# Layer 2's expert matrices: transposes one expert ahead with copies on ScalarE, and the second pair's answers added inside its own parts

## The chip, the cores and the metric

The kernel runs on one core of one Trainium2 chip. A core has five engines that matter here: TensorE (PE in the profile; PEld is its weight load), VectorE (DVE), ScalarE (ACT), GpSimd (POOL) and SyncE (SP), which here only issues transfers. The metric is the device time of one execution in microseconds (us), given as the median of several runs.

## The reference

Four layers work on one array x of 2048 tokens with 128 numbers each, seen as four blocks of 512 tokens. Each layer is a "macaron": half of a mixture of experts, an attention, half of the same mixture again, each on a normalized x and added to x. The change touches the seam between the second mixture of layer 0 and the first of layer 1, and a matrix product that prepares layer 2.

```python
x = x + 0.5 * _L0_ffn_ref(_layernorm(x), ...)      # 8 experts, one per token
x = x + 0.5 * _L1_ffn_ref(_layernorm(x), ...)      # 8 small experts, 2 per token, and a shared one
x = x + _L1_attn_ref(_layernorm(x), ...)
x = x + 0.5 * _L2_ffn_ref(_layernorm(x), ...)
```

Layer 2's experts have no nonlinearity between their two matrices: `h = xt @ w_in[e].T` and then `gates[:, e] * (h @ w_out[e].T)`. The two matrices of an expert can therefore be multiplied once, `w_in[e].T @ w_out[e].T`, to a single 128 x 128 matrix, and the mixture needs only that.

## The kernel before, in words

A token row of 128 numbers lies in one SBUF partition; a block of 512 tokens is a tile of 128 partitions by 4 rows. Layer 0's experts gather their tokens by transfers through DRAM, compute, and send each weighted answer row back to a DRAM array `res` with indirect transfers from GpSimd (`experts`, lines 418 to 523). `combine(b)` (lines 525 to 532) then loads the answers of block b from there with one transfer on SP into a tile of tag `n` of the pool `work`, which has three buffers, and adds them to x on VectorE.

Layer 1's mixture works on pairs of blocks. `l1_ffn` (line 1078) first calls `normed_T` (line 1042): `norms` takes the statistics of eight tiles of 128 tokens on VectorE (lines 160 and 161), the inverse root on GpSimd as a power (line 165), and the normalization alternately on VectorE (line 178) and ScalarE (line 174), into two tiles of the same tag `n`. TensorE transposes them (line 187, tile T_f), ScalarE copies the result out (nT_f, line 1049). Then follow the gate's logits (line 1058), the products with the up matrices (lines 1092 and 1093), the sigmoid on ScalarE (line 1096), two multiplications on VectorE (lines 1097 and 1098), the choice of two experts per token as a row of small VectorE operations (`route`, lines 216 to 226, and lines 1104 to 1115), the transposed gates (line 1071), their way through DRAM (lines 1075 and 1124), a multiplication by them on GpSimd (line 1147) and the down products (line 1135). `followed` puts behind the first pair's mixture the start of layer 1's attention for block 0.

`prep_l2` loads layer 2's weights and builds the eight expert matrices `m`. Its loads are issued one expert at a time during layer 0's experts, into a tile `raw` that fills with both matrices of all experts. After the experts' last product, its last part runs: for each expert four transposes of 128 x 128 into one PSUM bank (line 1275), a copy of 128 x 512 out of it (wo2T, line 1277), four accumulating products (line 1280) into another bank, and a copy of 128 x 128 into `m` (line 1283). Both copies go through a helper, `copy` (lines 131 to 136), that alternates between VectorE and ScalarE from call to call. The pool that holds `raw` ends with this part, so what is later placed in its room waits for the last product: GpSimd's memset of `vpad` (line 574) is the first such.

The order of the work has two sources. Where a block of code stands under `manual_schedule`, the four compute engines keep the order of the code: all of layer 1's attention is so written. Outside of it, as here, a planner lays out each engine's instructions in advance: it prefers what comes first in the code, and fills an engine that it reckons idle with later work that it reckons ready, by its own estimate of durations. On the chip each engine then keeps that order. `skewed(gens, lag)` (line 1468) sets the order of the code: in each round it takes one part of every generator, and the generator number i joins in round i x lag.

Of the kernel before, what the change touches and what calls it, by code (L numbers as in the profile page):

```python
# [9 lines left out]
FP = mybir.dt.float32  # L10
# [7 lines left out]
P = 128  # L18
D = 128
NB, S = 4, 512  # L20
# [3 lines left out]
E = 8  # L24
# [4 lines left out]
FF = 512  # L29
NC = FF // P  # L30
# [11 lines left out]
def kernel(ctx: ExitStack, tc: tile.TileContext, a: dict, out: bass.AP):  # L42
    nc = tc.nc
# [9 lines left out]
    def const(shape, name, dtype=FP):  # L53
        return cpool.tile(shape, dtype, name=name, tag=name)

    def bank(name):
        return psum.tile([P, 512], FP, name=name, tag="bank", bufs=8)
# [14 lines left out]
    ident = const([P, P], "ident")  # L72
# [46 lines left out]
    def load(ap, shape, name):  # L119
        t = pools["w"].tile(shape, FP, name=name, tag=name)  # L120
        nc.sync.dma_start(t, ap)
        return t

    def load_row(ap, name, tag=None):
        t = pools["w"].tile([P, D], FP, name=name, tag=tag or name)
        nc.sync.dma_start(t, ap.partition_broadcast(P))
        return t
# [3 lines left out]
    def copy(dst, src):  # L131
        n_copies[0] += 1
        if n_copies[0] % 2:
            nc.vector.tensor_copy(dst, src)
        else:
            nc.scalar.copy(dst, src)

    def load_T(ap, rows, cols, name, tag=None):

        dst = pools["w"].tile([cols, rows], FP, name=name, tag=tag or name)  # L140
        m = min(rows, P)
        k = rows // m
        raw = stage.tile([m, k, cols], FP, name=f"raw_{name}", tag="raw")
        nc.sync.dma_start(raw, ap.rearrange("(k m) c -> m k c", m=m))
        ps = bank(f"ps_{name}")
        for i in range(k):
            nc.tensor.transpose(ps[:cols, i * m : (i + 1) * m], raw[:, i, :], ident[:m, :m])
        copy(dst, ps[:cols, :rows])
        return dst
# [422 lines left out]
    def padded(pool, i):  # L572
        v = pool.tile([P, NT, NH, SLOT], FP, name=f"vpad{i}", tag=f"vpad{i}", bufs=1)
        nc.gpsimd.memset(v, 0.0)
        nc.gpsimd.memset(v[:, :, :, HD : HD + 1].rearrange("p t h o -> p (t h o)"), 1.0)
        return v
# [668 lines left out]
    def prep_l2(pool):  # L1245

        l2["gate"] = load_T(a["L2_ffn_w_gate"], E, D, "gate2T")
        l2["w_in"] = load(a["L2_attn_W_in"], [P, 2 * D], "win2")
        l2["w_out"] = load(a["L2_attn_W_out"], [P, D], "wout2")
        l2["b_out"] = load_row(a["L2_attn_b_out"], "bout2")  # L1250
        l2["b_in"] = load_T(a["L2_attn_b_in"].rearrange("(k d) -> k d", k=2), 2, D, "bin2T")
        yield

        m = pools["w"].tile([P, E, D], FP, name="m2", tag="m2")
        l2["m"] = m
        got = {}

        def fetch(e):
            wi, wo = raw[:, 0, e].rearrange("p (c d) -> p c d", d=D), raw[:, 1, e]
            nc.sync.dma_start(wi, a["L2_ffn_w_in"][e].rearrange("(c f) d -> f c d", f=P))  # L1260
            nc.sync.dma_start(wo, a["L2_ffn_w_out"][e])
            got[e] = wi, wo

        raw = pool.tile([P, 2, E, FF], FP, name="raw2", tag="raw2")
        for e in range(E):

            behind = yield
            nc.gpsimd.tensor_copy(raw[0:1, :, e, 0], behind[0:1, 0:1].to_broadcast([1, 2]))
            fetch(e)
        yield  # L1270
        for e in range(E):
            wi, wo = got[e]
            ps = bank(f"wo2T_{e}")
            for c in range(NC):
                nc.tensor.transpose(ps[:, c * P : (c + 1) * P], wo[:, c * P : (c + 1) * P], ident)
            woT = pool.tile([P, FF], FP, name=f"wo2T_{e}", tag="woT", bufs=3)
            copy(woT, ps)
            pm = bank(f"m2_{e}")
            for c in range(NC):
                nc.tensor.matmul(  # L1280
                    pm[:, :D], wi[:, c, :], woT[:, c * P : (c + 1) * P], start=(c == 0), stop=(c == NC - 1)
                )
            copy(m[:, e, :], pm[:, :D])

    def l2_ffn(pool, i, bs):
        tag = f"f2{i}_{bs[0]}"
# [95 lines left out]
    def prep_l3_ffn(behind):  # L1382
        l3["w"] = yield from moe_weights("L3_ffn", "l3", behind)
        l3["gate"] = wpool.tile([P, E], FP, name="gate3", tag="gate3")
        nc.sync.dma_start(l3["gate"], a["L3_ffn_wg"])
# [78 lines left out]
    def whole(parts):  # L1464
        for _ in parts:
            pass

    def skewed(gens, lag):

        live = {i: g for i, g in enumerate(gens)}  # L1470
        r = 0
        while live:
            for i in list(live):
                if r >= i * lag and next(live[i], "end") == "end":
                    del live[i]
            r += 1
            yield
# [19 lines left out]
    pairs = [[b, b + 1] for b in range(0, NB, 2)]  # L1497
    gate0T = wpool.tile([D, E], FP, name="gate0T", tag="gate0T")
    ps = bank("gate0T")
    nc.tensor.transpose(ps[:, :E], gate0, ident[:E, :E])  # L1500
    nc.vector.tensor_copy(gate0T, ps[:, :E])
    with tc.tile_pool(name="tables", bufs=1) as tables:
# [17 lines left out]
        f01 = Mixture("f01", CAP0, 1)  # L1520
# [3 lines left out]
    with tc.tile_pool(name="weights12", bufs=1) as mid:  # L1524
        pools["w"] = mid
        prep_l1()
        with tc.tile_pool(name="raw2", bufs=1) as pool:
            made = prep_l2(pool)
            next(made)
            next(made)  # L1530
            f01.experts(l0["w"], made.send)
            whole(made)
        first = small.tile([P, 1], FP, name="first_sigmoid", tag="first_sigmoid", bufs=1)
        nc.scalar.activation(first, l2["m"][:, 0, 0:1], AF.Sigmoid)
        for b in range(NB):
            whole(f01.combine(b))
        with tc.tile_pool(name="ahead1", bufs=2) as ahead:
            vpads[:] = [padded(ahead, 0), None]
            begun = l1_begin(ahead)

            def followed(pool, bs):
                yield from l1_ffn(pool, 0, bs)
                if bs[0] == 0:

                    yield from begun[0](0)
                    for g in range(2):
                        begun[1](0, g)
                        yield
                        begun[4][0, g] = begun[2](0, g)

            with tc.tile_pool(name="ffn10", bufs=2) as pool:
                whole(skewed([followed(pool, bs) for bs in pairs], 12))

            l1_attn(lambda pool: prep_l3_ffn(xs[0]), begun)

        def behind(pool, bs):
            yield from l1_ffn(pool, 1, bs)
            yield from l2_ffn(pool, 0, bs)
            yield from l2_attn(pool, bs)
            yield from l2_ffn(pool, 1, bs)  # L1560
            if bs[0] == 0:

                parts = f30.tokens(bs, l3["gate"], "scalar", pool, apart=True)
                while next(parts, "end") != "end" and next(parts, "end") != "end":
                    yield
            else:
                yield from skewed([f30.tokens([b], l3["gate"], "scalar", pool) for b in bs], 3)

        with tc.tile_pool(name="chain", bufs=2) as pool:
            decay = pool.tile([P, S], FP, name="decay", tag="decay", bufs=1)  # L1570
            nc.gpsimd.memset(decay, 0.9)
            for bs in pairs:
                l2["gates", bs[0]] = pool.tile([P, 2 * NT, P], FP, name=f"gates{bs[0]}", tag=f"gates{bs[0]}", bufs=1)
                nc.gpsimd.memset(l2["gates", bs[0]], 0.0)

            l2["row"] = []
            for u in range(E // 4):
                flag = pool.tile([P, 1], FP, name=f"flag{u}", tag=f"flag{u}", bufs=1)
                nc.vector.tensor_reduce(flag, ident.rearrange("p (r c) -> p r c", c=SLOT)[:, :, u], AX.X, ALU.add)
                row = pool.tile([P, P], FP, name=f"row{u}", tag=f"row{u}", bufs=1)  # L1580
                nc.vector.tensor_copy(row, flag.to_broadcast([P, P]))
                l2["row"].append(row)
            with tc.manual_schedule(engines={mybir.EngineType.Pool}):
                whole(skewed([behind(pool, bs) for bs in pairs], 8))
        pools["w"] = wpool
# [54 lines left out]
```

## Time and profile before

| | us |
|---|---|
| median of the timed runs | 1533.77 (1532.04 to 1535.4, 3 runs) |
| the profiled execution | 1513.06 |
| its span, first to last instruction | 1511.3 |
| TensorE busy in the span | 1271.2 (84%) |
| VectorE / ScalarE / GpSimd busy | 880.3 / 682.8 / 694.0 |
| stretch from layer 0's last product to T_f, 419.6 to 443.5 | 23.9 |
| TensorE / VectorE / ScalarE busy in it | 12.93 / 14.06 / 6.15 |

The profile shows one execution. Its times count from the first instruction; a group or a chain piece is named by engine, the tile that it writes and the line of the kernel. "Idle before" is the time in which the engine had nothing running ahead of an instruction, with what released it. The mean TensorE clock granted over the span was 0.911 of full speed, and 1.00 in the stretch from 419.6 to 443.5.

### The profile page before, as it was taken

What the parts mean: (1) busy time and instruction counts of PE and PEld (TensorE: products, weight loads), DVE (VectorE), ACT (ScalarE), POOL (GpSimd) and SP (SyncE); (2) the same over time, 40 slices, a digit from 0 to 9 for tenths busy, and PEclk for the clock granted to TensorE, in tenths of its full rate; (3) what the DMA queues carried; (4) which work ended last, traced back from release to release, by engine and by line L of the source; (5) the groups of instructions that cost most, each with busy time, mean ns of one, the idle gap of its engine ahead of it and who ended that gap; (6) DMA issues with size and microseconds to landing.
All of it is one profiled execution on the core that took longest, in us unless ns stands there. A gap on an engine that the chain in (4) does not pass through costs nothing.

```text
span 1511.3 us, 28774 instructions
## 1 busy us (share of the span) xinstructions
PE 1271.2 (84%) x10645; PEld 816.7 (54%) x10645; DVE 880.3 (58%) x2890; ACT 682.8 (45%) x1431; POOL 694.0 (46%) x808
## 2 busy tenths in 40 slices
PE   4787999995969999999878878729689999998394
PEld 3465666774746666667555656616433333333173
DVE  5236767763355657767456566525367787774343
ACT  1235877871422367767522222103236655564042
POOL 5346767871433678868323111464431223312343
PEclk9897999995999999999999888759879999999597
DMA  9410240002513884231022000023105000000223
GB/s 262 101 53 22 79 170 12 9 7 73 151 37 65 223 258 145 87 121 44 4 64 49 1 1 1 28 71 91 60 15 177 15 7 10 14 3 15 78 78 112
DMA packets 100660, 106.21 MB, mean 70 GB/s; under 512 B 9084, under 2 KB 73832, under 8 KB 100520
## 3 DMA queue, kind: packets, MB, share of 16 engines
q1 hardware_dynamic: 91752, 90.11, 20.7%
q0 software_dynamic: 6656, 13.22, 2.5%
q8 instruction: 84, 1.38, 0.4%
q10 hardware_dynamic: 2112, 1.05, 0.3%
q14 instruction: 56, 0.46, 0.1%
HBM read 62.49 MB, written 41.85 MB: 69 GB/s over the span
## 4 chain that ended last, share of the span: by engine, by line
PE 70%; DVE 9%; POOL 8%; DMA 5%; issue 5%; ACT 3%; SPq 1%; POOLq 0%; ACTq 0%; DVEq 0%
PE s_a L610 13%; PE t_a L655 10%; PE o_f L515 6%; PE h_f L479 6%; PE acc_a L677 5%; PE acc_a L749 5%; PE y_f L1329 3%; PE t_a L610 3%; POOL disp_f L408 2%; PE ot_a L768 2%; PE gu_f L1092 2%; PE lg_f L322 1%; POOL rstd_f L165 1%; DVE low L699 1%; PE gu_f L1093 1%
## 5 line engine op out<-in xcount | busy, mean ns | idle before, releaser
L642 POOL TENSOR_SCALAR sc_a<-sc_a,top_a 128x128 f32<-128x128 f32 (+3 forms) x256 | 274.8, 1089 | 84.7 <-DVE top_a L627 55.8
L610 PE MATMUL s_a<-k_a,q_a 32*128 32x512 f32 (+3 forms) x1536 | 263.4, 544 | 7.0 <-DVE top_a L631 3.7
L719 ACT ACTIVATE w_a<-t_a 128x512 f32<-128x512 f32 x256 | 140.4, 595 | 116.6 <-PE t_a L610 86.9
L699 DVE TENSOR_REDUCE low<-s_a 128x1 f32<-128x512 f32 x256 | 163.4, 684 | 45.4 <-PE t_a L610 32.7
L655 PE MATMUL t_a<-ident,sc_a 128*128 128x128 f32 x1280 | 174.3, 283 | 4.3 <-DVE top_a L631 3.8
L610 PE MATMUL t_a<-ql_a,k_a 32*128 32x512 f32 x512 | 167.2, 644 | 0.3 <-DVE low L699 0.2
L501 POOL DMA_INDIRECT res_f<-y_f,back_f x112 | 109.8, 980 | 124.6 <-ACT y_f L500 90.3
L655 PEld LDWEIGHTS t_a<-ident,sc_a 128*128 128x128 f32 x1280 | 144.6, 144 | 41.0 <-issue 16.5
L644 ACT ACTIVATE sc_a<-sc_a,top_a 128x128 f32<-128x128 f32 (+3 forms) x256 | 135.0, 575 | 12.8 <-DVE top_a L631 12.2
L610 PEld LDWEIGHTS s_a<-k_a,q_a 32*128 32x128 f32 x1536 | 91.5, 187 | 79.1 <-issue 41.9
L664 ACT ACTIVATE w_a<-t_a 128x256 f32<-128x256 f32 (+2 forms) x192 | 94.2, 526 | 71.0 <-PE t_a L655 70.8
L408 POOL DMA_INDIRECT disp_f<-n_f,to_f x96 | 94.8, 988 | 56.2 <-issue 35.8
L515 PE MATMUL o_f<-w_l,h_f 128*128 128x128 f32 (+1 forms) x896 | 109.6, 277 | 0.0
L515 PEld LDWEIGHTS o_f<-w_l,h_f 128*128 128x128 f32 (+1 forms) x896 | 102.1, 184 | 8.0 <-DVE back_f L464 4.4
L479 PE MATMUL h_f<-dT_f,w_l 128*128 128x320 f32 (+1 forms) x256 | 104.1, 544 | 2.8 <-ACT dT_f L457 2.8
L677 PE MATMUL acc_a<-w_a,vpad 128*32 128x128 f32 x2560 | 98.2, 280 | 0.0
L666 ACT COPY w_a<-t_a 128x256 f32<-128x256 f32 (+2 forms) x192 | 93.5, 527 | 5.0 <-PE t_a L655 4.7
L631 DVE CUSTOM_DVE_ANT_0 sc_a<-s_a,future 128x128 f32<-128x128 f32 (+3 forms) x128 | 62.3, 487 | 47.7 <-PE s_a L610 39.0
L1147 POOL TENSOR_TENSOR h_f<-h_f,cb_f 128x512 f32<-128x512 f32 x32 | 40.7, 1286 | 104.4 <-DVE h_f L1098 62.7
L631 DVE CUSTOM_DVE_ANT_0 sc_a<-s_a,table 128x128 f32<-128x128 f32 (+3 forms) x128 | 62.3, 487 | 43.5 <-PE s_a L610 38.3
L500 ACT ACTIVATE y_f<-o_f,d_f 128x128 f32<-128x128 f32 (+1 forms) x112 | 39.0, 394 | 98.0 <-DVE o_f L495 94.1
L749 PE MATMUL acc_a<-w_a,vpad 128*32 128x256 f32 x1024 | 82.1, 391 | 1.0 <-DVE low L699 0.9
(341 smaller groups left out, 2182.8 us busy)
## 6 DMA issues: line engine op xcount, KB each, us to landing
fac_a<-fac_a_sb SPq DMA_DIRECT2D x36, 256.0 KB, 4.9
disp_f<-zeros_f SPq DMA_DIRECT2D x4, 2080.0 KB, 10.6
d_f<-disp_f SPq DMA_DIRECT2D x32, 260.0 KB, 3.0
w_l<-in_L_ffn_w_dram SPq DMA_DIRECT2D x16, 512.0 KB, 7.2
cb_f<-rows_f SPq DMA_DIRECT2D x16, 512.0 KB, 8.4
q_a<-fac_a SPq DMA_DIRECT2D x32, 256.0 KB, 3.5
k_a<-fac_a SPq DMA_DIRECT2D x32, 256.0 KB, 3.8
r_f<-res_f SPq DMA_DIRECT2D x16, 256.0 KB, 2.8
```

The source lines that it names most:

```text
L408: nc.gpsimd.indirect_dma_start(out=self.to[c][i0 + t][:, :], out_offset=bass.IndirectOffsetOnAxis(ap=to[:, c, t : t + 1], axis=0), in_=ns[ ...
L479: nc.tensor.matmul(ps[u][:, :cap], w1[:, e, (c + u) * P : (c + u + 1) * P], dT, start=True, stop=True)
L515: nc.tensor.matmul(po[:m, s, :], h[:, c, s * P : s * P + m], w2[:, e, c, :], start=(c == 0), stop=(c == NC - 1),)
L610: nc.tensor.matmul(ps[:, n0:n1], q[r : r + SLOT, i * P : (i + 1) * P], k[r : r + SLOT, n0:n1], start=True, stop=True)
L631: nc.vector.tensor_tensor_reduce(sc, banks[r][:, :n], more, -1.0, HUGE, ALU.add, ALU.min, top)
L642: nc.gpsimd.tensor_scalar(sc, sc, top, None, ALU.subtract)
L644: nc.scalar.activation(sc, sc, AF.Exp, bias=top, scale=-1.0)
L655: nc.tensor.transpose(ps[:, x * n + j * P : x * n + (j + 1) * P], st["sc", u, i, r0 + x][:, j * P : (j + 1) * P], ident,)
L677: nc.tensor.matmul(st["acc", u][r * SLOT : (r + 1) * SLOT, i * P : (i + 1) * P], vpads[b % 2][:, j, g * 4 + r, :], st["w", u, i, r][:, j * ...
L699: nc.vector.tensor_reduce(st["low", u][:, i, c : c + 1], ps, AX.X, ALU.max, negate=True)
L719: nc.scalar.activation(w, ps, AF.Exp)
L749: nc.tensor.matmul(acc[r * SLOT : (r + 1) * SLOT, n0:n1], vpads[b % 2][:, j, g * 4 + r, :], st["w", u, j, r][:, n0:n1], start=(j == 0 and ...
```

## The change

Two edits. In `prep_l2`, the loop runs one round more than there are experts. In round e it transposes expert e's matrix and copies it, and then forms the product of expert e - 1. The code order on TensorE is thus T0, T1, P0, T2, P1, ... where it was T0, P0, T1, P1. Both copies are called on ScalarE directly and no longer go through the alternating helper.

In the main part, `combine` runs ahead of layer 1 for the first pair of blocks only. The second pair's two `combine` calls become the first two parts of its own generator `followed`, and the lag of the second generator goes from 12 rounds to 10, so that its `l1_ffn` begins in round 12, as before.

```diff
-        for e in range(E):
-            wi, wo = got[e]
-            ps = bank(f"wo2T_{e}")
-            for c in range(NC):
-                nc.tensor.transpose(ps[:, c * P : (c + 1) * P], wo[:, c * P : (c + 1) * P], ident)
-            woT = pool.tile([P, FF], FP, name=f"wo2T_{e}", tag="woT", bufs=3)
-            copy(woT, ps)
-            pm = bank(f"m2_{e}")
-            for c in range(NC):
-                nc.tensor.matmul(
-                    pm[:, :D], wi[:, c, :], woT[:, c * P : (c + 1) * P], start=(c == 0), stop=(c == NC - 1)
-                )
-            copy(m[:, e, :], pm[:, :D])
+        wT = {}
+        for e in range(E + 1):
+            if e < E:
+                ps = bank(f"wo2T_{e}")
+                for c in range(NC):
+                    nc.tensor.transpose(ps[:, c * P : (c + 1) * P], got[e][1][:, c * P : (c + 1) * P], ident)
+                wT[e] = pool.tile([P, FF], FP, name=f"wo2T_{e}", tag="woT", bufs=3)
+                nc.scalar.copy(wT[e], ps)
+            if e > 0:
+                pm = bank(f"m2_{e - 1}")
+                for c in range(NC):
+                    nc.tensor.matmul(
+                        pm[:, :D], got[e - 1][0][:, c, :], wT[e - 1][:, c * P : (c + 1) * P],
+                        start=(c == 0), stop=(c == NC - 1),
+                    )
+                nc.scalar.copy(m[:, e - 1, :], pm[:, :D])
...
-        for b in range(NB):
+        for b in pairs[0]:
             whole(f01.combine(b))
...
             def followed(pool, bs):
+                if bs[0] > 0:
+                    for b in bs:
+                        yield from f01.combine(b)
                 yield from l1_ffn(pool, 0, bs)
...
-                whole(skewed([followed(pool, bs) for bs in pairs], 12))
+                whole(skewed([followed(pool, bs) for bs in pairs], 10))
```

## The prediction

> **What bounds the kernel now.** I read the chain of waits first, cut to the stretch around the change, because a share over 1511 us says nothing on 24 of them. Columns: start, length, piece (all in us).
>
> ```profile
> 437.43 0.47 issue
> 437.89 1.13 PE m L1280 x8
> 439.02 0.44 PE wo2T L1275 x4
> 439.46 2.90 issue
> 442.36 1.13 PE m L1280 x8
> 443.49 0.45 PE T_f L187 x4
> ...
> 450.10 3.83 issue
> 453.93 1.29 PE gT_f L1071 x8
> ```
>
> The path that sets the end goes through layer 2's last two expert products (m). Behind them on TensorE stand the first pair's transposes (T_f), with which layer 1 starts. The 2.90 us of "issue" are a wait that the chain can't name, so I next read VectorE in order of time over the same stretch (start, length, instruction; in brackets the idle time before it and its releaser).
>
> ```profile
> 428.91 0.68 DVE L531 TENSOR_TENSOR x<-x,r_f 128x512 f32<-128x512 f32 x1
> ...
> 430.29 0.69 DVE L531 TENSOR_TENSOR x<-x,r_f 128x512 f32<-128x512 f32 x1 [0.22 <-DMA r_f<-res_f]
> 430.89 0.68 DVE L134 COPY wo2T<-wo2T 128x512 f32<-128x512 f32 x1
> ...
> 435.49 1.11 DVE L178 TENSOR_SCALAR n_f<-x,mv_f,rstd_f 128x128 f32<-128x128 f32 x4 [1.52 <-POOL rstd_f L165]
> ...
> 437.13 0.66 DVE L134 COPY wo2T<-wo2T 128x512 f32<-128x512 f32 x1
> ...
> 441.31 0.35 DVE L178 TENSOR_SCALAR n_f<-x,mv_f,rstd_f 128x128 f32<-128x128 f32 x1 [2.33 <-POOL rstd_f L165]
> 441.57 0.68 DVE L134 COPY wo2T<-wo2T 128x512 f32<-128x512 f32 x1
> ```
>
> The last copy of a transposed matrix (441.57) stands behind a normalization of the *second* pair (441.31), which waited 2.33 us for GpSimd's power. TensorE had finished those transposes at 439.46. The first pair's normalized rows were complete long before: VectorE's four at 436.6, ScalarE's four at 435.77 + 1.65 = 437.42. So T_f starts 5.9 us later than its own input allows. Third, the stretches: length, then busy us of each engine, then TensorE's clock, DMA share and GB/s.
>
> ```profile
> 419.60:443.50 23.90, 12.93 (x100) 11.09 (x99) 14.06 (x51) 6.15 (x16) 7.03 (x11) 1.00 0.17 51
> 443.50:454.00 10.50, 6.42 (x33) 3.95 (x32) 7.14 (x23) 3.53 (x8) 3.10 (x4) 1.00 0.01 2
> 454.00:515.80 61.80, 59.96 (x294) 38.78 (x293) 34.45 (x73) 15.43 (x27) 24.06 (x20) 0.97 0.58 150
> ```
>
> In the first, TensorE stands idle 11 of 23.9 us while ScalarE works 6.15. In the third it is busy 59.96 of 61.80: whatever moves T_f forward moves this whole block and the attention behind it, whose order on four engines is written out by hand.
>
> [...] the trace has 681 ns for wo2T's copy on VectorE and 588 ns for ScalarE's nT_f copies of the same shape, so I use 0.59. [...] the load here took 1283 ns at 422.57 and the next activation began 1.30 us after that start, so only the load is charged.
>
> **The change part by part, on the profiled execution** (1513.06 us, span 1511.3; the median of the timed runs, 1533.77, lies 20.7 above, and I carry the difference over unchanged).
>
> *Transposes ahead, copies on ScalarE.* Counts stay: 32 transposes, 32 products, 16 copies. Eight copies of 0.68 = 5.4 us leave VectorE and cost ScalarE 8 x 0.59 = 4.7; the eight small ones (0.26) were on ScalarE already. The helper that alternates engines is called 16 times fewer, an even number, so later copies keep their engine. ScalarE then holds 6.15 + 4.7 = 10.9 us in the stretch, and that is its cover: with none, it would cost 4.7.
>
> TensorE first. Transposes of expert 0 start at 419.66 as now. ScalarE is free from its last answer at 420.48, so copy 0 ends at 421.09 and product 0 starts about 421.15. One product and one transpose set take from 421.10 to 422.69 in the trace, 1.59 us. Inside that time the next copy (0.59) and the small one (0.26) fit, so no wait is left per expert. Product 7 starts at 421.15 + 6 x 1.59 + 0.99 = 431.7. The sigmoid table load (1.28 + 0.20) falls right behind the first m copy at 422.57 and holds copy 2 until 424.1 + 0.6; product 2 would start at 424.33, so 0.4 is lost. Product 7: 432.1 to 433.3, against 442.36 to 443.5.
>
> *Second pair's answers in its own parts.* In code order the adds for blocks 2 and 3 move behind ten rounds of the first pair; two rounds go to the adds and the lag falls from 12 to 10, so the second pair's layer starts in round 12 as now. Moved are two SP loads (256 KB, 2.8 us to landing), two VectorE adds (0.68) and, following them, eight tiles of statistics and normalization. SP stands empty from 427.8 to the row store at 455.17, so the loads pass nothing while they stay ahead of that.
>
> First pair's path now: answers land 426.7; two adds 0.69 + 0.67 = 428.1; eight tiles of statistics at 0.26 (433.07 less 432.04 for four) = 430.1. From the last statistic to ScalarE's first normalization the trace takes 435.77 - 433.16 = 2.6, to 432.75; its four take 1.65, to 434.4. It also has the last copies in that time (0.59 + 2 x 0.26 = 1.1), in an order that the planner draws up from its own estimates: T_f's input is ready at 434.4 to 435.5. Product 7 itself may stand behind the four normalizations: copy to 435.1, product to 436.3. So T_f starts between 434.5 and 436.4. I take 435.4, since it orders by code position and only the last copies are near. Against 443.22 that is 7.8 us.
>
> *What is late next.* The second pair's VectorE work, 1.4 of adds + 2.1 of statistics + 1.4 of normalization = 4.9 us, and its share on ScalarE (4 x 0.41), were hidden under TensorE's wait and must go elsewhere. VectorE is next needed at 447.29 - 7.8 = 439.5 and free from about 433.9: 5.6 us of room, with a GpSimd power (2.3 with its surroundings) in the middle. From 447.3 to 453.9 VectorE is the path: TensorE's 3.83 us wait for the routing. Lower bound 0 (all fits in the room, or behind 455, where VectorE is half idle), upper bound 4.9 + 2.3. I take 0.8. These results aren't needed until the second pair's transposes at 474.81, so late is harmless; only standing in front hurts.
>
> Sum: -7.8 + 0.8 = -7.0. Profiled 1506.1, median 1526.8.
>
> **Rivals.** *1. The second pair's norm lands in the routing chain.* For: today's order shows such filling (statistics at 436.52 ahead of a ready copy), and the planner evidently reckons the power short. Against: in code order it now stands behind the routing. Adding 4 of the 7.2 us gives 1533.77 - 7.8 + 4 = 1530.0.
>
> *2. The product chain still ends late,* ScalarE's normalizations taking VectorE's part as blockers of two copies instead of one: products 6 and 7 behind 434.4 + 2 x 0.59, then 2 x 0.99 of products with waits between, T_f about 438.2, 1533.77 - 5.0 + 0.8 = 1529.6. The same if only half the change acts.
>
> *3. Slower: the fourth load waits for a buffer.* Answers and normalized rows share three buffers. If block 3's load gets one only after T_f (ends 436.4) and VectorE has the add and the norm queued ahead of the first gated product: landing 439.2, add and four statistics 441.0, GpSimd's three memsets and mask (3.3) first, power 2.6, normalization 1.7: 448.6 against 447.29 now, 1.3 slower: 1535.1. It decides once that norm ends after 447.3. Against: before 436 buffers are freed by the adds (block 3's load went out 0.03 us after the first add ended, at 427.43), and nothing forces the norm ahead.
>
> **Chances.** Likeliest case 0.68; rivals 1 and 2 0.13 each; rival 3 0.06. A measurement of this kernel tells 0.2%, about 3.1 us, from no change. Rival 1 crosses that line in a third of its cases and rival 3 goes beyond it on the slow side half the time: faster 0.89, same 0.08, slower 0.03. The likeliest case alone spans 1524.5 to 1529.0 (T_f's bounds 434.5 to 436.4, 0 to 2 of crowding, and the 1.7 us by which a timed run strays from the median). The range takes in both rivals and a little upside from an order with shorter waits in the routing: 1523.3 to 1531.
>
> **What would show it.** Right: wo2T's copies on ScalarE, eight of about 0.59; the last m product near 433, T_f within 2 us of it; VectorE showing only two adds of answers before the first pair's power; TensorE's stretch of 60 busy us starting about 446.5. Wrong: ScalarE's copies waiting behind GpSimd's power; a wait on r_f or on the second pair's power ahead of the gated products (L1097) or the routing; the 3.83 us wait at the routing grown; a block that starts earlier but ends no earlier than 508.

## The result, and the profile after

The changed kernel takes 1525.55 us in the median (1517.6 to 1535.01, 20 runs), beside 1531.82 us for the kernel before on the same chip: a ratio of 0.9961 [0.9945, 0.9976], or 6.0 us less [3.7, 8.4]. The forecast was 1526.8, 7.0 less. The times agree better than the working behind them does, so the rest goes by the stretch around the change.

One thing first. The profiled execution of the changed kernel has a *longer* span, 1518.4 us against 1511.3. TensorE's instructions stand in the same order outside the changed stretch, so the two traces can be laid side by side instruction by instruction: the changed kernel leads by 8.2 us near 957 us, and then loses 4.1 us at 965 to 988 and 3.8 at 1380 to 1437, with smaller pieces between, where both do the same work. A second pair of executions, on another chip, has 1511.0 before and 1506.6 after. Spans of two single executions don't tell a gain of this size; the stretch does.

Not all of the lead of 8.2 us is the stretch's. 0.9 was there before it, and 2.9 came behind it, between the attention's start at 516 and 957, in instructions that stand in the same order on TensorE in both kernels (2.5 in the second pair). Part of this is TensorE's clock: sixteen transposes of the attention (t_a) took 3.62 us at 0.50 of full speed before and 2.59 at a mean of 0.73 after. The kernels "answers only" and "not ahead" below gain 5.6 and 5.7 us there with next to nothing gained in the stretch, so a timed difference can hold more than the stretch. Why the clock falls differently there is open.

The chain of waits after (start, length, piece), to be laid beside the one of before:

```profile
433.60 1.16 PE m L1283 x8
434.76 0.45 PE T_f L187 x4
...
441.37 6.47 issue
447.84 1.87 PE gT_f L1071 x8
```

The last product ends near 434.6, the first pair's transposes (T_f) follow at once, at 434.60 in the list of TensorE's instructions, and the wait at the routing has grown from 3.83 to 6.47 us. The stretches (length, busy us of TensorE, weight load, VectorE, ScalarE, GpSimd, then clock, DMA share, GB/s) say who works in that wait:

```profile
434.60:441.37 6.77, 6.52 (x34) 4.02 (x32) 2.64 (x8) 2.76 (x6) 2.96 (x4) 1.00 0.14 41
441.37:447.84 6.47, 0.00 (x1) 0.03 (x1) 4.53 (x26) 0.30 (x1) 2.33 (x4) 0.88 0.00 0
447.84:510.50 62.66, 60.83 (x290) 39.14 (x291) 35.06 (x76) 16.66 (x31) 24.07 (x20) 0.96 0.58 147
```

VectorE is busy 4.53 of the 6.47 and GpSimd 2.33: the wait is theirs. VectorE in order of time:

```profile
439.68 0.69 DVE L1098 TENSOR_TENSOR h_f<-h_f,gu_f 128x512 f32<-128x512 f32 x1 [0.25 <-PE gu_f L1093]
440.29 0.22 DVE L220 TENSOR_TENSOR eq<-sc_f,mx 128x64 f32<-128x64 f32 x1
440.42 0.69 DVE L531 TENSOR_TENSOR x<-x,r_f 128x512 f32<-128x512 f32 x1
...
444.75 0.18 DVE L161 BATCH_NORM_AGGREGATE mv_f<-st_f 128x2 f32<-128x6 f32 x1
...
445.12 0.22 DVE L1114 SCALAR_TENSOR_TENSOR comb_f<-comb_f,sc_f 128x64 f32<-128x64 f32 x1
447.26 0.34 DVE L178 TENSOR_SCALAR n_f<-x,mv_f,rstd_f 128x128 f32<-128x128 f32 x1 [1.91 <-POOL rstd_f L165]
447.52 0.22 DVE L1115 TENSOR_TENSOR comb_f<-comb_f,total_f 128x64 f32<-128x64 f32 x1
```

Block 3's answers are added at 440.42, in the middle of the routing; their statistics last until 444.9; only then does GpSimd begin on the power, at 445.01, and the second pair's normalization (447.26), which waits 1.91 us for it, stands in front of the routing's very last operation. Counted by starts, the second pair's own work in this row is 2.0 us, and with the wait 3.9. One reason for the late addition stands in SP's queue, in the answer on what its loads waited for (us in total, times, longest):

```profile
SPq L530 <- DVE n_f L178: 4.5, 1, 4.5
SPq L530 <- PE T_f L187: 2.8, 1, 2.8
```

One of the four loads of answers waited for the first pair's normalization, the last one for T_f itself, which frees a buffer of tag `n`. The loads were issued from 423.04 to 435.63, where the last had gone out by 427.80 before. The other reason is the planned order. The transfer of block 3's answers was over by 437.8, and VectorE stood idle until 438.61; the addition, put behind four other operations, came 1.8 us later.

Since the first additions of answers start at slightly different times (426.71 before, 425.83 after), the tables below count from that addition.

| from VectorE's first addition, us | T_f | L1097 | routing's end (L1115) | wait before gT | gT | attention's first product |
|---|---|---|---|---|---|---|
| before | 16.62 | 20.58 | 26.90 | 3.84 | 27.22 | 89.05 |
| after | 8.77 | 12.78 | 21.69 | 6.48 | 22.01 | 84.67 |

T_f comes 7.8 us earlier, as forecast. At the routing 5.2 of it is left, at the attention 4.4.

### The profile page after: what moved, and what is told of

The parts are those of the page before. It is cut to its first block, busy times and chain, and to the rows that moved or that the text cites. A ratio compares the mean times of both kernels' runs of the same rounds, so it can differ in the third digit from the quotient of the medians.

```text
span 1518.4 us, 28780 instructions
## 1 busy us (share of the span) xinstructions
PE 1273.5 (84%) x10645; PEld 816.0 (54%) x10645; DVE 872.5 (57%) x2882; ACT 686.1 (45%) x1439; POOL 694.4 (46%) x808
## 3 DMA queue, kind: packets, MB, share of 16 engines
q10 hardware_dynamic: 2112, 1.05, 0.3%
## 4 chain that ended last, share of the span: by engine, by line
PE 66%; DVE 9%; POOL 9%; issue 7%; DMA 5%; ACT 3%; SPq 1%; POOLq 0%; ACTq 0%; DVEq 0%
PE s_a L610 13%; PE t_a L655 9%; PE h_f L479 5%; PE acc_a L677 5%; PE o_f L515 5%; PE acc_a L749 5%; PE y_f L1333 3%; PE t_a L610 3%; POOL disp_f L408 2%; PE gu_f L1092 2%; PE ot_a L768 2%; PE gu_f L1093 2%; POOL res_f L501 2%; PE gate_f L1350 1%; PE o_f L1135 1%
## 5 line engine op out<-in xcount | busy, mean ns | idle before, releaser
L1147 POOL TENSOR_TENSOR h_f<-h_f,cb_f 128x512 f32<-128x512 f32 x32 | 40.7, 1287 | 97.0 <-DVE h_f L1098 61.5
```

## The experiments

All of the runs together, with the same measures; where the two halves of T_f start apart, both starts are given. Ratios are to the kernel before on the same chip, which took 1532.0 us on the chip of the first four and 1512.8 on that of the others; only ratios compare between them.

| run | T_f | L1097 | wait before gT | gT | attention | ratio |
|---|---|---|---|---|---|---|
| matrices only | 7.82, 9.99 | 15.21 | 3.16 | 24.47 | 86.25 | 0.9969 [0.9957, 0.9982] |
| answers only | 14.74 | 18.70 | 4.89 | 26.39 | 88.87 | 0.9984 [0.9970, 0.9999] |
| copies on vector | 11.49 | 18.07 | 4.26 | 28.31 | 93.16 | 0.9999 [0.9985, 1.0013] |
| not ahead | 15.73 | 19.85 | 3.85 | 26.46 | 88.92 | 0.9994 [0.9976, 1.0011] |
| before again | 16.60 | 20.56 | 3.84 | 27.21 | 89.14 | one execution |
| own buffers | 9.96 | 14.43 | 4.52 | 21.70 | 83.72 | 0.9969 [0.9956, 0.9981] |
| tensor kept busy | 9.54 | 14.02 | 1.33 | 23.25 | 86.16 | 0.9973 [0.9956, 0.9990] |
| own buffers, kept busy | 9.96 | 16.20 | 0.75 | 25.70 | 90.74 | 0.9977 [0.9962, 0.9993] |
| after again | 9.28 | 14.09 | 6.47 | 23.32 | 85.77 | 0.9984 [0.9970, 0.9997] |
| filled | 8.76 | 12.77 | 6.66 | 22.18 | 85.45 | 0.9968 [0.9953, 0.9984] |
| own buffers, filled | 9.09 | 18.59 | 3.28 | 28.03 | 90.48 | 1.0005 [0.9990, 1.0021] |
| own buffers, last copy on vector | 7.21, 9.38 | 14.59 | 4.24 | 23.68 | 85.79 | 0.9978 [0.9966, 0.9990] |

The left columns are one execution each, the ratio 13 to 22 runs. Most intervals overlap each other: the ratios tell most versions from before, few from one another.

**Each edit alone.** First the matrices' edit without the answers' edit, from the changed kernel:

```diff
-        for b in pairs[0]:
+        for b in range(NB):
             whole(f01.combine(b))
...
-                if bs[0] > 0:
-                    for b in bs:
-                        yield from f01.combine(b)
...
-                whole(skewed([followed(pool, bs) for bs in pairs], 10))
+                whole(skewed([followed(pool, bs) for bs in pairs], 12))
```

> The matrices' edit alone; all four blocks' answers are added ahead of layer 1 and the lag is 12, as before. Clocked from the first addition of answers to the attention's first product, the kernel before took 89.05 us and the changed one 84.67; from that addition to the first pair's transposes 16.5 and 8.8. Theory A (the product chain held the transposes, and the second pair's additions in front of the statistics cost only their own 1.4 us): transposes at 10.2 us, TensorE's wait at the routing about 3.8 us as before since block 3's answers come early, so the whole stretch 83 us, shorter than with both edits. Rival B (the answers' edit is what frees the transposes): transposes not before 13 us, stretch 86 us or more.

Measured: T_f begins at 7.82, earlier than in the full change, but its second half comes only at 9.99, and L1097 at 15.21 against 12.78. VectorE, in order of time:

```profile
437.65 2.49 DVE L178 TENSOR_SCALAR n_f<-x,mv_f,rstd_f 128x128 f32<-128x128 f32 x4 [1.91 <-POOL rstd_f L165]
...
444.56 0.35 DVE L178 TENSOR_SCALAR n_f<-x,mv_f,rstd_f 128x128 f32<-128x128 f32 x1 [2.91 <-POOL rstd_f L165]
445.44 0.69 DVE L1097 TENSOR_TENSOR h_f<-h_f,gu_f 128x512 f32<-128x512 f32 x1 [0.53 <-ACT h_f L1096]
```

The first pair's four normalizations take 2.49 us instead of 1.11 (the last part says beside what), which cuts T_f in two. The second pair's normalization (444.56) waits 2.91 us for its own power and stands in front of the first gated product. TensorE's granted clock was also at 0.50 from 438.5 to 452.2. So the delay has three causes here, which this run does not separate. In this execution the matrices' edit alone brings 2.8 of the change's 4.4 us at the attention; a stretch of 83 was expected and 86.25 measured.

Then the answers' edit alone, on the kernel before:

```diff
-        for b in range(NB):
+        for b in pairs[0]:
             whole(f01.combine(b))
...
             def followed(pool, bs):
+                if bs[0] > 0:
+                    for b in bs:
+                        yield from f01.combine(b)
...
-                whole(skewed([followed(pool, bs) for bs in pairs], 12))
+                whole(skewed([followed(pool, bs) for bs in pairs], 10))
```

> The answers' edit alone; matrices as before, copies alternating. Theory A: eight copies still stand in VectorE's queue between statistics and normalizations, a product and its transposes keep their pace of 2.4 us, transposes of the first pair at 13 us after the first addition, stretch 86 to 87 us. Rival B: transposes at 10 us or earlier, and most of the 4.4 us of the stretch gained: 85 us.

Measured: T_f 14.74 and the attention at 88.87, where T_f near 13 and 86 to 87 were expected. Of the 1.9 us won at T_f 0.8 are left at gT, with a wait at the routing of 4.89, and 0.2 at the attention. The product chain keeps VectorE's copies and with them its pace.

**Which half of the matrices' edit.** The full change with the large copies on VectorE, and the full change with the transposes not ahead:

```diff
-                nc.scalar.copy(wT[e], ps)
+                nc.vector.tensor_copy(wT[e], ps)
```

> The changed kernel with the eight large copies on VectorE and the transposes still one expert ahead. If the order on TensorE alone does it: last product and transposes as in the changed kernel, 8.8 us after the first addition, stretch 84.7. Theory A (the engine matters, since VectorE's queue holds the statistics on the same path): the copies of experts 3 to 7 stand between additions, statistics and normalizations, transposes at 10.5 to 11 us, stretch about 86.5.

The loop of before, with both copies on ScalarE (the rest of the change kept):

```diff
-            copy(woT, ps)
+            nc.scalar.copy(woT, ps)
...
-            copy(m[:, e, :], pm[:, :D])
+            nc.scalar.copy(m[:, e, :], pm[:, :D])
```

> The changed kernel with both copies on ScalarE, but each expert's product right behind its own transposes in code order. Theory A (order and engine are both needed): a round of transposes 0.6, copy 0.7 and product 1.1 makes 2.4 us with nothing beside it, eight of them end 19 us after the first transposes, so the transposes of the first pair come at 12 us after the first addition, stretch 87 to 88. If the engine alone does it: 8.8 and 84.7.

With neither half (answers only) T_f is at 14.74. The order alone brings it to 11.49, the engine alone to 15.73, both to 8.77; the ratios of the two halves have intervals that hold 1. At the attention copies on vector reach 93.16 (86.5 was expected) and not ahead 88.92 (87 to 88). Not ahead (12 was expected for T_f), every expert pays for its copy in TensorE's time. Ahead with VectorE's copies the products finish earlier than in the change, and another queue is then late. GpSimd and VectorE of that run:

```profile
434.87 1.80 POOL L574 MEMSET vpad<- 128x2048 f32 x1 [10.28 <-PE m L1283]
...
438.31 1.68 POOL L165 TENSOR_TENSOR rstd_f<-rs_f,mhalf 128x8 f32<-128x8 f32 x1
```

```profile
434.43 0.30 DVE L161 BATCH_NORM_AGGREGATE mv_f<-st_f 128x2 f32<-128x6 f32 x2
440.02 1.12 DVE L178 TENSOR_SCALAR n_f<-x,mv_f,rstd_f 128x128 f32<-128x128 f32 x4 [5.29 <-POOL rstd_f L165]
```

The statistics, with copies between them, end at 434.7, and the memset of `vpad`, which waits in GpSimd's queue for the last product, has just been released in front of the power. The normalization waits 5.29 us.

**Is the shared buffer what makes the second pair late?** The second pair's answers go into tiles of the pool `stage`, tag `raw`, instead of tag `n`:

```diff
-        def combine(self, b):
+        def combine(self, b, pool=None):
...
-                r = work.tile([P, NT, D], FP, name=f"r{j}{b}_{self.tag}", tag="n", bufs=3)
+                if pool is None:
+                    r = work.tile([P, NT, D], FP, name=f"r{j}{b}_{self.tag}", tag="n", bufs=3)
+                else:
+                    r = pool.tile([P, NT, D], FP, name=f"r{j}{b}_{self.tag}", tag="raw")
...
-                        yield from f01.combine(b)
+                        yield from f01.combine(b, stage)
```

> The changed kernel, but the second pair's two loads of answers go into buffers of another pool (tag raw of the staging pool, idle here) and not into the three shared with the normalized rows, so block 3's load needn't wait for the first pair's transposes. Theory A (the late load is what puts block 3's addition, statistics and the wait for the second pair's power into the routing): the addition comes 6 to 8 us after the first one and not 14.6, TensorE's wait at the routing falls from 6.48 to about 4.3 us, stretch from the first addition to the attention 84.67 to about 82.4 us. Rival (the planner's order does it, whatever the buffer): wait 6 us or more, stretch 84.7.

SP's loads no longer wait for anything but the answers themselves:

```profile
SPq L533 <- DMA res_f<-y_f,back_f: 10.2, 3, 7.8
```

The two additions come at 3.36 and 4.03 instead of 6.96 and 14.59, the power ends before the routing needs VectorE, and the row from L1097 to L1115 takes 6.95 instead of 8.91 us. Its normalization waits for nothing:

```profile
429.67 0.66 DVE L534 TENSOR_TENSOR x<-x,r_f 128x512 f32<-128x512 f32 x1
...
441.88 0.34 DVE L178 TENSOR_SCALAR n_f<-x,mv_f,rstd_f 128x128 f32<-128x128 f32 x1
```

So without the shared buffer the longer row is gone. The edit did two things at once, though: it let the load go early, and it changed where the planner put additions and statistics. The kernel "filled", below, tells them apart. And the same kernel loses on the other side, in TensorE's list:

```profile
433.73 2.08 PE L1286 MATMUL m<-wo2T,raw 128*128 128x128 f32 x8 [4.12 <-ACT wo2T L1282]
435.60 1.73 PE L187 MATMUL T_f<-ident,n_f 128*128 128x128 f32 x8
```

Product 7 waits 4.12 us for a copy that stands behind a normalization on ScalarE, TensorE's clock falls to 0.50 from 433.6 on for 3.4 us, and product and transposes take almost twice the 1.06 and 1.04 us that they take elsewhere. T_f is at 9.96, 1.2 later than in the change. At the attention 0.95 us are left (83.72; 82.4 was expected), or 2.05 against the second execution of the changed kernel, below.

**Does TensorE's low clock behind the routing cost anything?** In the changed kernel gT and its neighbours run at clock 0.50. Six products that nothing reads are put into the wait at the routing, and, in a second kernel, four of them with the answers in their own buffers:

```diff
         up(0, 1)
+        if i == 0 and bs[0] == 0:
+            unread = bank("unread")
+            for _ in range(6):
+                nc.tensor.matmul(unread, ident, nTs[0], start=True, stop=True)
         yield
```

> The changed kernel with six products of 128x512 more (0.86 us each, 5.2 in all) into an unread bank, right behind the first pair's second gate and up products, where TensorE waits 6.48 us for the routing. Theory C (a long wait also halves TensorE's granted clock for the 5 us behind it): the clock stays 1.00 behind the wait, the 5.2 us that ran at 0.50 take about 2.6 us, stretch 84.67 to about 82.1 us, at no cost since the added products fit in the wait. Rival (the clock behind the wait is of no consequence, or falls in any case): stretch 84.7 or more.

> Own buffers for the second pair's answers and four products of 128x512 more (3.4 us) in the then shorter wait at the routing. If the two causes are separate: wait near 4.3 us, filled but for 0.9, clock 1.00 behind it, stretch 80.5 us, against 89.05 before and 84.67 in the changed kernel. If they are one (the clock falls only because the wait is long): no shorter than own buffers alone, 82.4 us.

TensorE in the first of them:

```profile
442.97 5.31 PE L1120 MATMUL unread<-nT_f,ident 128*128 128x512 f32 x12
449.61 1.03 PE L1071 MATMUL gT_f<-ident,comb_f 128*8 128x128 f32 x8 [1.33 <-issue]
450.48 1.02 PE L1092 MATMUL gu_f<-nT_f,wg1T 128*128 128x512 f32 x2
```

The clock held at 1.00: gT takes 1.03 us instead of 1.87, a pair of gated products 1.02 instead of 1.9. Still, from gT to the attention it is 62.91 us against 62.66, and the attention is at 86.16, where 82.1 was expected. Another chain holds the end behind the routing: gates to DRAM and back, then GpSimd's multiplications by them (L1147). TensorE reached the products behind these early and waited 0.30 and 0.99 us for them. From the first multiplication to the attention's first product lie 51.2 us before and 51.2 after, and 51.0 to 51.6 in ten of the other twelve runs (54.5 in the second kernel here, 52.2 in "filled").

That chain begins with ScalarE's copy out of gT, and there another of the second pair's instructions stands in front. ScalarE, before and after:

```profile
454.56 1.27 ACT L1073 COPY gT_f<-gT_f 8x512 f32<-8x512 f32 x2 [4.70 <-PE gT_f L1071]
```

```profile
447.54 1.65 ACT L174 ACTIVATE n_f<-x,off_f,rstd_f 128x128 f32<-128x128 f32 x4 [6.40 <-POOL off_f L169]
449.09 1.23 ACT L1073 COPY gT_f<-gT_f 8x512 f32<-8x512 f32 x2
```

The copy starts 0.63 us behind gT before and 1.25 after, because the second pair's four normalizations on ScalarE waited for the late power too. With the six products in the wait it is 1.25 as well, so this run can't show what the clock would be worth at that place. Where nothing stands in front, the copy starts 1.05 behind gT at half clock (own buffers) and 0.64 at full (the second kernel here), and the first multiplication comes 10.88 and 10.53 behind it: about 0.4 us.

The second kernel, for which 80.5 was expected and 90.74 measured, loses in other places: its clock was at 0.50 from 434.6 to 448.3, before its fillers, L1097 came at 16.20, and behind the first multiplication TensorE waited 2.01 us for GpSimd at a place where the changed kernel has no wait.

**The same kernels again.** The kernel before and the changed kernel, for how far one execution can be trusted:

> The kernel before once more, for a second profile of it: how far the stretch from the first addition of answers to the attention's first product (89.05 us) and TensorE's clock in it differ from execution to execution. If the stretch is set by the order of the instructions alone: 89.0 within 0.3 us. If the granted clock is a draw: up to 3 us off.

> The changed kernel once more, beside the three that follow. Times are counted from VectorE's first addition of answers. If the late block is the cause and not chance: T_f at 8.8 again (8.6 to 9.6, since the granted clock at T_f may differ), block 3's addition at 14 to 16, TensorE's wait at the routing 6 to 6.6, the attention's first product near 84.7. If the longer wait at the routing came from that one execution: wait back near 4 and the attention's first product near 82.

Before again agrees within 0.1 us in every column. After again has the same long wait at the routing, the addition of block 3 at 15.91 and ScalarE's copy 1.25 behind gT, but reaches T_f and L1097 later, 0.5 and 1.3 us:

```profile
431.94 1.65 PE L1283 MATMUL m<-wo2T,raw 128*128 128x128 f32 x8 [3.43 <-ACT wo2T L1279]
433.38 1.92 PE L187 MATMUL T_f<-ident,n_f 128*128 128x128 f32 x8
...
447.42 1.87 PE L1071 MATMUL gT_f<-ident,comb_f 128*8 128x128 f32 x8 [6.47 <-issue]
```

T_f takes 1.92 us for what took 1.04: behind the longer wait ahead of product 7 the clock fell, at 432.45. On this chip the change gives 0.9984 [0.9970, 0.9997], 2.4 us less [0.5, 4.5], and the stretch 3.4 us instead of 4.4. The two intervals overlap only from 3.7 to 4.5 us, so the 6.0 of the first comparison are probably in part chance, or the chips differ.

**Can the clock be kept up ahead of T_f?** Unread products between products 6 and 7: two in the changed kernel, four with the answers in their own buffers.

```diff
+                if e == E:
+                    unread = bank("unread")
+                    for _ in range(2):
+                        nc.tensor.matmul(unread, ident, wT[e - 2], start=True, stop=True)
                 pm = bank(f"m2_{e - 1}")
```

> The change with two products more, whose results nothing reads, between layer 2's products 6 and 7, where TensorE waits 2.3 us. Theory A (the clock at T_f is worth up to 0.8 us per execution, but the second pair's normalization in front of the routing sets the stretch): clock 1.00 from product 7 through T_f in every look, T_f at 8.8, L1097 at 12.8, wait at the routing 6.5 as before, attention's first product 84.3 to 84.9. Theory B (the half clock of the transposes carries through to the end): in the timed runs 0.8 us less than the change.

> Second pair's answers in buffers of their own and, in the wait of 4.1 us ahead of product 7, four unread products of 0.86 us. Theory A (buffers and clock are two separate losses that add up): T_f 9.96 to 9.0, L1097 14.4 to 13.2, gT 21.7 to 20.4, attention's first product 83.7 to 82.5; 1.5 to 2 us less than the change. Theory B (the routing is bound by VectorE's own row, so an earlier T_f only lengthens the wait at the routing): gT stays at 21.5 to 21.9.

In the first the clock stayed at 1.00 through T_f, T_f and L1097 are where the better of the two executions of the changed kernel had them, and the wait at the routing is 6.66; the attention is at 85.45, where 84.3 to 84.9 was expected. Here block 3's load waited for VectorE only, not for T_f. VectorE:

```profile
437.73 0.69 DVE L531 TENSOR_TENSOR x<-x,r_f 128x512 f32<-128x512 f32 x1 [1.64 <-DMA r_f<-res_f]
438.45 0.29 DVE L160 BATCH_NORM_STATS2 st_f<-x 128x6 f32<-128x128 f32 x1
439.97 0.69 DVE L1097 TENSOR_TENSOR h_f<-h_f,gu_f 128x512 f32<-128x512 f32 x1 [1.22 <-ACT h_f L1096]
...
447.38 0.34 DVE L178 TENSOR_SCALAR n_f<-x,mv_f,rstd_f 128x128 f32<-128x128 f32 x1 [1.85 <-POOL rstd_f L165]
```

The addition comes at 10.53, ahead of L1097. VectorE then stands idle for 1.22 us with the rest of the statistics ready to run (0.9 us of them), but in its order they stand behind L1097, inside the routing, and the normalization there still waits 1.85 us for the power. So with the data there in time the row from L1097 to L1115 is as long as in the changed kernel (9.09 against 8.91 us): what lengthens it is the planned order. The shared buffer matters where taking it away changes that order, as with own buffers. How the planner reckoned is not on record. That the filler pays in the timed runs can't be said: 0.9968 and 0.9984 have overlapping intervals.

The second has the highest ratio of all, 1.0005, and not through its four products. ScalarE's list, and TensorE's:

```profile
440.10 0.88 ACT L174 ACTIVATE n_f<-x,off_f,rstd_f 128x128 f32<-128x128 f32 x2 [3.32 <-POOL off_f L169]
440.88 0.24 ACT L1294 COPY m<-m 128x128 f32<-128x128 f32 x1
441.03 1.07 ACT L1052 COPY nT_f<-T_f 128x512 f32<-128x512 f32 x2
```

```profile
436.51 1.04 PE L187 MATMUL T_f<-ident,n_f 128*128 128x128 f32 x8
441.66 1.77 PE L1061 MATMUL lg_f<-gate1T,nT_f 128*128 128x8 f32 x8 [4.12 <-ACT nT_f L1052]
```

With the fillers in the program the planner places two of the second pair's normalizations ahead of the copies that T_f's result waits for. They wait 3.32 us for the power, TensorE waits 4.12, and its clock is at 0.50 from 441.8 to 452.1. T_f was 9.09 as expected; L1097 comes 4.2 and gT 6.3 us later than with own buffers alone.

**Last copy on VectorE.** The answers in their own buffers, and one copy moved:

```diff
-                nc.scalar.copy(wT[e], ps)
+                (nc.vector.tensor_copy if e == E - 1 else nc.scalar.copy)(wT[e], ps)
```

> Buffers of their own as before and the copy of the last transposed matrix alone on VectorE, where it stands ahead of the first normalization, so that it no longer queues on ScalarE behind normalizations that wait for GpSimd's power. Theory A (product 7 late is what delays T_f there): product 7 near 5, T_f with the normalized rows at 8.7 to 9.3, gT 20.3 to 21, attention's first product 82.5 to 83.2. Theory B (TensorE idle 3 us longer ahead of T_f runs at half clock for longer behind it): T_f 9.3 but L1097 still at 14.4 and gT at 21.7 or later.

Product 7 came at 5.35 and the first half of T_f at 7.21, but the second half at 9.38, L1097 at 14.59 and gT at 23.68. The last product ends at 432.48, before the normalizations begin, and GpSimd's memset, which in the changed kernel waited 2.87 us for that product, runs beside them:

```profile
432.78 2.49 DVE L178 TENSOR_SCALAR n_f<-x,mv_f,rstd_f 128x128 f32<-128x128 f32 x4 [1.51 <-POOL rstd_f L165]
433.24 1.88 POOL L577 MEMSET vpad<- 128x2048 f32 x1 [0.22 <-DVE n_f L178]
435.35 1.09 PE L187 MATMUL T_f<-ident,n_f 128*128 128x128 f32 x4 [0.89 <-DVE n_f L178]
```

The four normalizations take 2.49 us instead of 1.11, T_f is cut in two, and the clock was at 0.50 from 433.8 to 444.0. The attention is at 85.79, where 82.5 to 83.2 was expected. The half clock lasts longer than in own buffers (10.2 against 3.4 us), as the expectation's second theory had it; that an emptier TensorE is the reason is not shown, since ahead of T_f's first half it waited 1.28 and 0.70 us here and 4.12 there. That the memset is a second part of it is read from the trace alone.

No version that was run is shown to beat the changed kernel. Own buffers has the earliest attention, 83.72, and 0.9969 [0.9956, 0.9981] against 0.9984 [0.9970, 0.9997] on the same chip; that is not resolved.

## Why the prediction was right, and where it was not

*Transposes ahead, copies on ScalarE* (term -7.8): right in size and mechanism. T_f moved from 16.62 to 8.77 behind the first addition, 7.8 us (7.3 in the second execution). Luck helped on the way: a round of one product and one transpose set was sized at 1.59 us and took 1.33 undisturbed, and the table load, which held product 2's copy, cost TensorE a wait of 1.65 where 0.4 was forecast. The two errors cancel: product 6 came 4.42 us behind the first addition, where 4.4 follows from the forecast. The two-by-two shows that order and engine are both needed (11.49 and 15.73 with one of them, 14.74 with neither, 8.77 with both). Without the answers' edit T_f began at 7.82 and L1097 still came at 15.21, with three causes not separated.

*Rival 2*, normalizations in front of copies on ScalarE, is true in mechanism and small in effect. Two normalizations stand in front of the last large copy:

```profile
432.04 0.49 ACT L174 ACTIVATE n_f<-x,off_f,rstd_f 128x128 f32<-128x128 f32 x1 [2.28 <-POOL off_f L169]
432.44 0.24 ACT L1287 COPY m<-m 128x128 f32<-128x128 f32 x1
432.58 0.49 ACT L174 ACTIVATE n_f<-x,off_f,rstd_f 128x128 f32<-128x128 f32 x1
432.98 0.57 ACT L1279 COPY wo2T<-wo2T 128x512 f32<-128x512 f32 x1
```

Product 7 waited 2.30 us for it and started 7.77 us behind the first addition, where 5.4 was forecast (432.1 less 426.7) and 8.4 allowed for (435.1). T_f lost little by it: the last of the four normalizations, its own input, ends at 434.49, and T_f starts at 434.60 behind product 7. The copies between the normalizations stretch these from 1.65 us to 2.45, so 0.8 us is the most that T_f can have lost.

*What is late next* (term +0.8): this is the step that failed. From T_f to gT the time grew by 2.6 us (10.60 to 13.24), and gT to the attention by another 0.8 (0.5 in the second execution). The room on VectorE was there: it stands idle for 3.88 us ahead of L1097. But block 3's answers landed only near its end, and their addition and statistics were planned behind it. Two sentences were wrong. Under rival 3: "before 436 buffers are freed by the adds". In the trace the last load waits for T_f. Under rival 1: "in code order it now stands behind the routing". The planner put it into the routing all the same, and in front of its last operation. Rival 1's order came true, together with rival 3's late load, at 2.6 us instead of their 4 and 9; the forecast's own sign of being wrong, a longer wait at the routing, was seen. Own buffers shows that the loss can be taken away: that row takes 2.0 us less. "Filled" shows that the planned order alone is enough for it: there the load is early, and the row stays long.

*The block of 60 busy us "moves whole"*: true of its start only in part. Of the 0.8 us lost behind gT, 0.6 is the later start of ScalarE's copy out of gT, behind the second pair's four normalizations. The forecast had named these ("its share on ScalarE (4 x 0.41)") among what must go elsewhere and gave them no price. "Busy 59.96 of 61.80" was read as the bound, and a clock of 0.97 as full. At the start of that block the clock is 0.50, and with it held at 1.00 TensorE only waited for GpSimd instead (0.30 and 0.99 us).

*The sum* was -7.0 against -4.4 and -3.4 in the two traces of the stretch and, timed, -6.0 [-8.4, -3.7] and -2.4 [-4.5, -0.5]. The sign holds in both timings, the range in the first; the second ratio, taken on the forecast's base of 1533.77, would be 1531.3, just past the range's upper end of 1531. The first timing's closeness to the forecast is luck as far as the term of 0.8 goes: the stretch gave 4.4 us, and part of what the timing shows beyond it can lie elsewhere in the kernel.

## What to carry to other kernels

Work that was hidden under a wait goes somewhere when the wait is taken away; before giving it a new place, follow its *input*: which buffer its load needs, who frees that buffer, and when, in the new order. Then follow its *place* in each engine's order, which a planner that works from estimates may choose badly even when the input is early: here the moved work brought 2.0 us of its own and a wait of 1.9 into VectorE's row, and 0.6 into ScalarE's, by standing in front of the wrong neighbour. And when an engine is almost fully busy, look at its clock before calling it the bound: here it was 0.50 for 3.41 of the 61.80 us.

## What the runs showed of the hardware

**TensorE's clock.** The traces of before and after have it at 1.00 or at 0.50 in each of their 42 stretches and at nothing between; other figures here are means. At 0.50 T_f (x8) takes 1.73 to 1.92 us instead of 1.04, a pair of 128x512 products 1.9 to 2.06 instead of 1.02 to 1.10. In these two traces every stretch but the last, at either clock, lasts 3.41 us or a whole multiple of it. Between 428 and 462 us every half-clock stretch of the fourteen traces lasts 3.41 us or two, three or four times as long, in the other twelve as far as windows of 2 and 4 us tell: 3.41 before (from 454.56), 6.83 after (446.31), 10.24 in "filled" (445.11), 13.65 in "matrices only" (438.51). What brings the clock down, the runs don't settle. Ahead of product 7 a wait of 2.30 us left the clock at 1.00, and behind waits of 3.43 and 4.12 it was at 0.50. But before the change waits of 2.25 and 2.90 left it at 1.00 in one execution, while in the other it fell behind the first of them (436.33); and in "matrices only" no wait longer than 1.52 came ahead of the fall. The changed kernel had T_f at full clock in one execution and at half in the next. The forecast had none of this; it is one reason why T_f to L1097 took 3.96 to 4.12 us in six executions and 4.5 to 6.2 in four others (own buffers, tensor kept busy, both together, after again).

**VectorE beside GpSimd's memset.** Four normalizations (128x128) take 1.11 us alone, and 2.49 with a memset of 1.88 to 1.91 us running, in three kernels (matrices only, own buffers filled, last copy on vector). The loss is 1.4 us, most of the memset; by what means the one holds up the other, the traces don't show. Before and after the change the memset waited 2.00 and 2.87 us for the last product and started behind the first pair's normalizations (at 443.55 and 434.87). In "matrices only" and "last copy on vector" that product had ended by 436.53 and 432.48, while GpSimd was still at the power, and the memset (from 438.09 and 433.24) ran beside the normalizations that T_f needs. So an earlier last product can slow these.
